# A two-layer graph kernel: plain stores in place of accumulating ones, the longest lists sorted in blocks, and the weights in a stream of their own

## The chip, the cores and the metric

The kernel runs on one core of a Trainium2 chip. The metric is the device time of one execution in microseconds (us); lower is better. A core has five engines with a queue each: TensorE (PE in the profile, with its weight loads as PEld), VectorE (DVE), ScalarE (ACT), GpSimd (POOL) and SyncE (SP). Plain transfers are issued here from SP, indirect ones (rows picked by a list of indices) from POOL.

## The reference

16 graphs of 1024 nodes with 64 channels. `adj` is a 1024 x 1024 matrix per graph with few entries; row and column i have weights that fall with i, so the first nodes have long neighbour lists.

```python
# layer 0
h = jnp.maximum(_layernorm(x, axis=-1), 0.0)
deg = jnp.clip(jnp.sum(A, axis=2, keepdims=True), 1.0, None)
x = x + jnp.matmul(A / deg, h)
# layer 1
h = jnp.maximum(_layernorm(x, axis=-1), 0.0)
adj_d = _dilate_adj(adj, mask)           # lists over 10 long lose two neighbours, both ways
vals = jnp.where(valid[..., None], h[:, None, :, :], big)
sv = jnp.sort(vals, axis=2)              # each channel sorted over a node's neighbours
# agg = 0.25 q(0.25) + 0.5 q(0.5) + 0.25 q(0.75), interpolated quantiles of sv
out = h + agg
y = relu(out @ W1 + b1) @ W2 + b2
x = x + y * mask
```

## The kernel before

The work has two parts. In the **layered part** each graph ("batch") is read once in eight row blocks `at` of 128 x 1024. ACT takes the sign of each block (`signs`), DVE finds neighbours with MAX8 (`listing`), PE transposes the block (`transposes`) and multiplies it with the normalised input (`products`). DVE then adds the input and leaves x after layer 0 in the tile `row`, at columns from `X1` on; `channels` normalises it into the first columns of `row`, stores the x part to `out` (16 stores of 256 KB) and the first 66 columns to a table `tab` in DRAM. `endings` sorts nodes by list length and scatters each row of `row`, without its x part (100 floats), to `srt`, by eight indirect DMAs per batch from POOL.

After every four batches, `group` reads the records of `srt`, cuts lists into classes by length (15, 10, 8, 7, 6, 5, 4, 3, 2, 1 neighbours at most) and makes a `Job` of each class, with T tiles of 128 nodes. After the last batch `long_lists` does the same for the four longest kinds (88, 31, 24 and 20 neighbours). This last stretch, with the last groups' jobs and the long lists, I call the **tail**.

A job goes like this. `run` issues on POOL one gather per list place and tile (`places<-tab,idx`, 128 rows of 66 floats; `lplaces` for long lists), and an SP load of the nodes' own rows (`S<-srt`). When all gathers are in, `sort` runs on DVE: it marks removed neighbours (`rem`, `gone`, `ok`), counts (`valid`), sets up the quantile weights (`q`, `u`), puts a huge value in the removed places, and runs a sorting network of MIN and MAX operations (`network` lists them, `spread` orders them); ACT finishes the weights (`wu`); DVE multiplies them in (`prod`). `layers` then sums the weighted places by PE transposes into `pt`, ACT copies to `ot`, PE multiplies with W1 (`ps_small`), ACT applies bias and ReLU (`hid`), PE multiplies with W2 and adds the bias `b2` by one more small matmul per tile, ACT multiplies by the mask into `y`, and POOL scatters `y` to `out`, one indirect DMA per tile that adds to what the plain stores left there. A chunk of `layers` holds up to four tiles; there are 128 tiles and 56 chunks in all. Between two scatters to the same tensor in a row a small memset (`turn`) is put on POOL.

Who comes next is set by a planner (`Plan`). Every piece of work is a generator ("stream") that yields the engine it needs next and the earliest time by the planner's own cost estimates; the planner always takes the stream that can begin first, with ranks for ties. What it yields is only a position: DVE and POOL execute exactly in the order in which the planner wrote their instructions, while the order on PE, ACT and SP is set by the compiling layer. `SLACK` (2) and `LOOSE` (7) are margins that the planner adds behind a result of another engine, as in the scatter of y:

```python
yield "POOL", lambda: at(y) + LOOSE
rows = out_rows[:min(self.g + 1, NG) * GB * N, :]
scatter(rows, y[:, t, :], self.nodes_i[:, t:t + 1], scatters, OP.add)
```

All recorded instructions have one line in the profile, L225, that of the recording helper; they are told apart by the names of their tiles.

Of the kernel before, what the change touches and what calls it, by code (L numbers as in the profile page):

```python
# [9 lines left out]
F32 = mybir.dt.float32  # L10
# [30 lines left out]
LSUB = 8  # L41
MOST = 8
# [106 lines left out]
def network(n, width):  # L149

    count = -(-3 * (n - 1) // 4) + 1
    live = set(range(count))
    layers = []
    for layer in reversed(SHORT.get(n) or batcher(n)):
        kept = [(i, j, i in live, j in live) for i, j in layer if i in live or j in live]
        live.update(x for pair in kept for x in pair[:2])
        layers.append(kept)  # L160
    goes = iter(GOES.get(n, ()))
    rules = iter(GOES_LONG.get(n, "").split())
    at = [2] + [0] * (n - 1)
    ops = []
    for layer in reversed(layers):
        kinds, after = {}, {}
        rule = dict(zip(sorted({(at[i], at[j]) for i, j, _, _ in layer}), next(rules, "")))
        for i, j, lo, hi in layer:
            ai, aj = at[i], at[j]
            other = (0 if ai == 1 else 1) + (0 if aj == 1 else 2)  # L170
            to = int(rule.get((ai, aj)) or next(goes, other))
            results = [(OP.min, i, to & 1)] * lo + [(OP.max, j, to >> 1)] * hi

            results.sort(key=lambda r: r[2] == at[r[1]])
            after.update({i: 0, j: 0})
            for turn, (op, x, copy) in enumerate(results):
                kinds.setdefault((turn, op == OP.max, ai, aj, j - i, copy), []).append(i)
                after[x] = copy
        for x, copy in after.items():
            at[x] = copy  # L180
        for (_, is_max, *kind), left in sorted(kinds.items()):
            cover = grids_of if rule else runs_of
            ops.extend((OP.max if is_max else OP.min, *kind, run) for run in cover(left))
    return spread(ops, width), count, at


def spread(ops, width):

    left, order = list(ops), []
    clock, ready = 0.0, {}  # L190
    while left:
        best, reads, writes = None, set(), set()
        for k, (op, ai, aj, dist, copy, run) in enumerate(left):
            run = numbers(run)
            near = {(ai, i) for i in run} | {(aj, i + dist) for i in run}
            out = {(copy, i + (dist if op == OP.max else 0)) for i in run}
            if not (near & writes or out & (reads | writes)):
                begin = max(clock, *(ready.get(key, 0.0) for key in near))
                if best is None or begin < best[0]:
                    best = begin, k, out  # L200
            reads |= near
            writes |= out
        begin, k, out = best
        clock = begin + 0.07 + len(numbers(left[k][5])) * width * 1.04e-3
        ready.update((key, clock + 0.15) for key in out)
        order.append(left.pop(k))
    return order
# [156 lines left out]
def list_path(ctx, tc, x, adj, nodemask, w1, b1, w2, b2, out, go):  # L364
# [12 lines left out]
    R0 = W  # L377
    X1 = RW = R0 + REC
# [64 lines left out]
    b2_sb = consts.tile([1, CO], F32, name="b2_sb")  # L443
    nc.sync.dma_start(b2_sb, b2.rearrange("(o c) -> o c", o=1))
# [110 lines left out]
    def beginnings(pool, now):  # L555

        for b, st in enumerate(batch):
            now[0] = b
            yield "DVE", lambda: max(known(st, "xt", "mrow"), room("h0", 3), room("row", 4))
            mrow_f = new(tiny, [NT, P], F32, "mrow_f", 2)  # L560
            nc.vector.tensor_copy(mrow_f, st["mrow"])

            h0 = new(pool, [P, NT, C + 1], F32, "h0", 3, users=2)
            nc.vector.memset(h0[:, :, C:], 1.0)
            row = st["row"] = new(pool, [P, NT, X1 + C], F32, "row", 4, users=1)
            nc.vector.memset(row[:, :, C:W], -1.0)
            yield from normed(h0[:, :, :C], st["xt"])
            st["h0"] = h0
            yield "PE", lambda: max(at(mrow_f), room("ps_small", 3))
            pm = new(ps_s, [P, HALF], F32, "ps_small", 3, users=1)  # L570
            nc.tensor.transpose(pm[:, :NT], mrow_f, ident[:NT, :NT])
            yield "ACT", lambda: at(pm)
            nc.scalar.copy(row[:, :, RW - 1], pm[:, :NT])
            nc.scalar.copy(row[:, :, RW - 2], row_f)
            free(pm)
# [79 lines left out]
    def products(pool, now):  # L655


        for b, st in enumerate(batch):
            now[0] = b
            for hf in range(2):  # L660
# [25 lines left out]
                x1 = st["row"][:, hf * BPH:(hf + 1) * BPH, X1:]  # L686
# [13 lines left out]
    def channels(pool, now):  # L700

        for b, st in enumerate(batch):
# [3 lines left out]
            yield from normed(row()[:, :, :C], row()[:, :, X1:])  # L706

            nc.sync.dma_start(out[b].rearrange("(t p) c -> p t c", p=P), row()[:, :, X1:])
# [5 lines left out]
    def endings(pool, now):  # L714

        first = lambda rank: rank - 3000
        for b, st in enumerate(batch):
# [55 lines left out]
            for t in range(NT):  # L773
                yield "POOL", lambda: max(at(to), at(row)) + LOOSE if "normed" in st else INF, first
                scatter(srt[g], row[:, t, :RW], to[:, t:t + 1], sorts[g])
# [10 lines left out]
    def scatter(dst, src, idx, others, op=OP.bypass):  # L786
        if plan.last is others:
# [3 lines left out]
            in_=src, in_offset=None, compute_op=op,  # L791
# [7 lines left out]
    class Job:  # L799
# [3 lines left out]
        def __init__(self, pool, n, T, keys, idx, node, mask, nodes_i, table, S, g, name="places",  # L803
                     bufs=4, rank=0):
            self.__dict__.update(locals())
            self.short = pool is gat

        def run(self):
# [10 lines left out]
            if short:  # L819
                mine = self.S  # L820
                self.S = new(pool, [P, T, W], F32, "S", 4, users=1)
                nc.sync.dma_start(self.S, mine)
            for t in range(T):
                for k in range(n - 1):
# [4 lines left out]
                    progress["ahead"] -= 1  # L829
            yield "DVE", lambda: max(  # L830
# [11 lines left out]

        def sort(self):
            n, T, pool, short, A, S = self.n, self.T, self.pool, self.short, self.A, self.S
            name = "" if short else "l"
            bufs = 2 if short else 1
            rem = new(pool, [P, n - 1, T, 2], F32, name + "rem2", bufs)
            nc.vector.tensor_tensor(
                rem, A[:, 1:, :, C:],
                self.node.unsqueeze(1).unsqueeze(3).to_broadcast([P, n - 1, T, 2]), OP.is_equal,  # L850
            )
            gone = new(pool, [P, n - 1, T], F32, name + "gone", bufs)
            nc.vector.tensor_tensor(gone, rem[:, :, :, 0], rem[:, :, :, 1], OP.max)
            ok = new(pool, [P, n - 1, T], F32, name + "ok", bufs)
            nc.vector.scalar_tensor_tensor(
                ok, self.keys.rearrange("p t k -> p k t"), 0.0, gone, op0=OP.is_gt,
                op1=OP.subtract,
            )
            valid = new(pool, [P, T], F32, name + "valid", bufs)
            nc.vector.tensor_reduce(valid, ok.rearrange("p k t -> p t k"), AX.X, OP.add)  # L860

            ops, count, copies = network(n, T * C)
            K = len(QUANTILES)
            q = new(pool, [P, K, T], F32, name + "q", bufs)
            nc.vector.tensor_tensor(
                q, taus.unsqueeze(2).to_broadcast([P, K, T]),
                valid.unsqueeze(1).to_broadcast([P, K, T]), OP.mult,
            )
            u = new(pool, [P, K, count, T], F32, name + "wu", 1)
            nc.vector.tensor_tensor(  # L870
                u, col_f[:, :count].unsqueeze(1).unsqueeze(3).to_broadcast([P, K, count, T]),
                q.unsqueeze(2).to_broadcast([P, K, count, T]), OP.subtract,
            )
            vals = A[:, 1:, :, :].rearrange("p k t w -> p (k t) w")[:, :, :C]
            nc.vector.scalar_tensor_tensor(
                vals,
                gone.rearrange("p k t -> p (k t)").unsqueeze(2).to_broadcast([P, (n - 1) * T, C]),
                HUGE, vals, op0=OP.mult, op1=OP.add,
            )
# [5 lines left out]
            yield "ACT", lambda: at(u) + SLACK  # L885
            nc.scalar.activation(u, u, AF.Abs)
            nc.scalar.activation(u, u, AF.Relu, bias=wt0, scale=-QUANTILES[0][1])
# [17 lines left out]
            begin = plan.clock["DVE"]  # L905
            for op, ai, aj, dist, copy, run in ops:
                each = numbers(run)
                near = [(ai, i) for i in each] + [(aj, i + dist) for i in each]
                soon = max(done.get(key, begin) for key in near)
# [15 lines left out]
            yield "DVE", lambda: at(u) + SLACK, self.later  # L925
# [38 lines left out]
        def layers(self, terms, sources):  # L964

            T, R = self.T, terms[0][0].shape[1]
            yield "PE", lambda: max(at(*sources) + LOOSE, room("y", 4), room("pt", 2))
            y = new(mlp, [P, T, CO], F32, "y", 4, users=1)
            for t0 in range(0, T, 4):
# [27 lines left out]
                pv = py[:, :len(ts) * CO].rearrange("p (t c) -> p t c", c=CO)  # L997
                for i, t in enumerate(ts):
                    nc.tensor.matmul(
                        pv[:, i, :], hid[:, i * P:(i + 1) * P], w2_sb, start=True, stop=False  # L1000
                    )
                    nc.tensor.matmul(pv[:, i, :], ones_f[:1, :], b2_sb, start=False, stop=True)
                yield "ACT", lambda: at(py) + SLACK
                for i, t in enumerate(ts):
                    nc.scalar.activation(
                        y[:, t, :], pv[:, i, :], AF.Copy, scale=self.mask[:, t:t + 1]
                    )
                free(py)
            for t in range(T):
                yield "POOL", lambda: at(y) + LOOSE  # L1010
                rows = out_rows[:min(self.g + 1, NG) * GB * N, :]
                scatter(rows, y[:, t, :], self.nodes_i[:, t:t + 1], scatters, OP.add)
# [3 lines left out]
    def group(g):  # L1016
# [107 lines left out]
        for i, ts in enumerate(classes):  # L1124
# [4 lines left out]
                nodes_i[:, sl], table, tiles[:, sl, :W], g,  # L1129
# [396 lines left out]
```

## Time and profile before

| | |
|---|---|
| median of 3 runs | 1586.0 us (1583.88 to 1586.02) |
| the profiled execution's own time | 1823.34 us |
| its span | 1821.4 us |
| granted TensorE clock in it | 0.653 |
| busy PE, DVE, ACT, POOL | 825.6, 1240.1, 609.3, 1050.8 us |
| indirect DMAs on POOL: gathers `places`, `lplaces` | 496 of 998 ns, 163 of 1049 ns |
| scatters to `srt`, to `out` | 128 of 1011 ns, 124 of 1678 ns and 4 of 1626 ns |
| last scatter to `srt` | begins at 988.4 us |

Groups of instructions in the profile read: line, engine, operation, output<-inputs, count, then busy us and mean ns of one, then the idle time of the engine just before them and what ended it. In the view of waits a line reads: who waited, for whom, us in total, times, longest. In the order of time: start, duration, engine, line, operation, and in brackets the idle time before it. The profiled execution takes longer than the timed runs; durations of single instructions are its own.

### The profile page before, as it was taken

The page shows a single profiled execution, that of the slowest core. Times are in us where ns is not written, and L with a number is a line of the kernel's source. Part 1 is how long each engine was busy: PE and PEld are TensorE (multiplying, and loading weights), DVE is VectorE, ACT ScalarE, POOL GpSimd, SP SyncE. Part 2 cuts the span into 40 slices and gives each one's busy share as a digit, 9 for nine tenths or more (in the row PEclk, how much of TensorE's full clock was granted, in tenths as well). Part 3 has the DMA queues.
Part 4 walks back from the last instruction along what each step waited for, and adds up shares of the span by engine and source line. Part 5 has one row for each costly group of instructions (what it writes and reads, how often), then busy time and mean ns, then how long its engine had stood idle before and what let it go on. Part 6 is the DMA issues. An engine that isn't in the chain of part 4 may idle for free. (4 is left out here: it accounts for less than half of the span.)

```text
span 1821.4 us, 15210 instructions
## 1 busy us (share of the span) xinstructions
PE 825.6 (45%) x3336; PEld 533.0 (29%) x3336; DVE 1240.1 (68%) x4046; ACT 609.3 (33%) x1874; POOL 1050.8 (58%) x1144
## 2 busy tenths in 40 slices
PE   5767822365686572563685000110031366253364
PEld 3333411233444341232354000100021245242343
DVE  7865858475788486678642889339497678896622
ACT  8877653245655464444442000000010111010011
POOL 0112263636467655555758766567656788575757
PEclk8978855675798675775885555555555567555656
DMA  5544741233444353353222211101111112111112
GB/s 170 163 133 122 199 125 31 48 101 81 121 134 112 58 134 91 90 138 73 56 48 49 43 43 34 23 17 22 28 24 28 18 26 20 23 30 23 24 18 17
DMA packets 147941, 124.89 MB, mean 69 GB/s; under 512 B 117715, under 2 KB 117843, under 8 KB 147843
## 3 DMA queue, kind: packets, MB, share of 16 engines
q1 hardware_dynamic: 102818, 86.58, 16.8%
q0 software_dynamic: 45024, 37.28, 12.2%
q14 instruction: 71, 0.57, 0.1%
q8 instruction: 28, 0.46, 0.1%
HBM read 104.51 MB, written 19.28 MB: 68 GB/s over the span
## 5 line engine op out<-in xcount | busy, mean ns | idle before, releaser
L225 POOL DMA_INDIRECT places<-tab,idx x496 | 495.0, 998 | 165.1 <-issue 140.2
L225 PE MATMUL pt<-ident,prod 128*128 128x128 f32 (+1 forms) x736 | 161.8, 384 | 569.4 <-DVE prod L225 294.5
L225 POOL DMA_INDIRECT out_dram<-y,nodes_i x124 | 208.0, 1678 | 186.8 <-ACT y L225 127.4
L225 PEld LDWEIGHTS pt<-ident,prod 128*128 128x128 f32 (+1 forms) x736 | 134.2, 267 | 605.3 <-issue 389.7
L225 POOL DMA_INDIRECT srt<-row,to x128 | 129.4, 1011 | 259.0 <-ACT row L225 223.5
L225 PE MATMUL pt<-ident,at 128*128 128x128 f32 x1024 | 190.0, 334 | 179.6 <-ACT att L225 72.1
L225 PE MATMUL ps_small<-att,h 128*65 128x512 f32 x512 | 259.0, 652 | 17.7 <-ACT h L225 10.3
L225 PEld LDWEIGHTS pt<-ident,at 128*128 128x128 f32 x1024 | 143.5, 171 | 236.5 <-ACT att L225 97.7
L225 POOL DMA_INDIRECT lplaces<-tab,lidx x163 | 171.0, 1049 | 49.7 <-issue 49.1
L225 ACT COPY att<-pt 128x512 f32<-128x512 f32 x256 | 142.9, 583 | 155.7 <-remote 84.2
L225 DVE MAX8 rec<-sg 128x8 f16<-128x256 f16 x512 | 180.1, 414 | 9.5 <-remote 5.2
L225 ACT ACTIVATE wu<-wu 128x39 f32<-128x39 f32 (+9 forms) x40 | 9.4, 234 | 431.7 <-DVE wu L225 168.8
L225 ACT ACTIVATE sg<-at 128x1024 f16<-128x1024 f32 x128 | 134.9, 1055 | 31.7 <-DMA at<-in_adj_dram 15.3
L225 DVE TENSOR_TENSOR sg<-sg,keyed 128x1024 f16<-128x1024 f16 x128 | 87.4, 683 | 65.5 <-issue 33.4
L225 PEld LDWEIGHTS ps_small<-att,h 128*65 128x65 f32 x512 | 75.4, 153 | 149.4 <-issue 126.5
L225 ACT COPY ot<-pt 128x128 f32<-128x128 f32 (+3 forms) x56 | 22.4, 400 | 246.7 <-remote 128.2
L225 PE MATMUL ps_small<-ot,w_sb 128*128 128x128 f32 (+3 forms) x112 | 55.9, 593 | 104.7 <-ACT ot L225 72.6
L225 PE MATMUL ps_small<-w_sb,hid 128*128 128x64 f32 x256 | 72.5, 376 | 52.6 <-ACT hid L225 25.1
L225 DVE TENSOR_TENSOR other<-places,other 128x64 f32<-128x64 f32 (+6 forms) x204 | 69.5, 341 | 35.6 <-remote 16.3
L225 PEld LDWEIGHTS ps_small<-w_sb,hid 128*128 128x128 f32 x256 | 53.6, 258 | 80.5 <-ACT hid L225 40.3
L225 DVE TENSOR_TENSOR rem<-places,recs 128x30 f32<-128x30 f32 (+9 forms) x40 | 7.3, 182 | 101.7 <-DMA places<-tab,idx 90.0
L225 POOL MEMSET turn<- 128x1 f32 x204 | 76.2, 373 | 0.1
(206 smaller groups left out, 1712.2 us busy)
## 6 DMA issues: line engine op xcount, KB each, us to landing
at<-in_adj_dram SPq DMA_DIRECT2D x128, 512.0 KB
places<-tab,idx POOLq DMA_INDIRECT x496
tab<-row SPq DMA_DIRECT2D x16, 264.0 KB
xt<-in_x_dram SPq DMA_DIRECT2D x16, 256.0 KB
out_dram<-row SPq DMA_DIRECT2D x16, 256.0 KB
lplaces<-tab,lidx POOLq DMA_INDIRECT x163
recs<-srt SPq DMA_DIRECT2D x4, 544.0 KB
srt<-row,to POOLq DMA_INDIRECT x128
```

Source lines behind the costliest of these rows:

```text
L225: ins = getattr(self._engine, op)(*args, **kwargs)
```

## The change

- The tile `row` and the sorted table `srt` now carry x after layer 0 as well (164 floats a row, was 100). The plain stores of `row` to `out` are gone.
- `layers` fetches x of its nodes: short jobs by an SP load from `srt` into the tile `y` (40 loads in all), long lists from their `S` tile. `y` has five buffers (was four).
- The last step moves from ACT to DVE: y = PSUM x mask + x in one operation per tile, and the scatter to `out` is a plain one. The bias `b2` comes by one matmul per chunk, of up to 256 columns, ahead of the W2 matmuls (one of 64 columns per tile behind each before).
- Lists of more than `BLOCK` (32) places, that is the longest kind, start their sort as a stream of its own, in blocks of 32 places: each block is prepared when its gathers are in (`prepared`), and network operations that stay in one block are kept apart.
- The two ACT operations for the weights become a stream of their own (`weigh`); the network no longer follows them in the planner's order.

The core of the diff:

```diff
-def network(n, width):
+def network(n, width, block=None):
...
+        apart = block and all(i // block == j // block for i, j, _, _ in layer)
...
+                kind = i // block if apart else 0, turn, op == OP.max, ai, aj, j - i, copy
+                kinds.setdefault(kind, []).append(i)
...
+    ready = {(0, i): 1.3 * block * (i // block + 1) for i in range(n)} if block else {}
+    return spread(ops, width, ready), count, at
...
-    R0 = W
-    X1 = RW = R0 + REC
+    X1 = W
+    R0 = X1 + C
+    RW = R0 + REC
...
-            nc.sync.dma_start(out[b].rearrange("(t p) c -> p t c", p=P), row()[:, :, X1:])
...
-                scatter(srt[g], row[:, t, :RW], to[:, t:t + 1], sorts[g])
+                scatter(srt[g], row[:, t, :], to[:, t:t + 1], sorts[g])
...
-                self.S = new(pool, [P, T, W], F32, "S", 4, users=1)
-                nc.sync.dma_start(self.S, mine)
+                self.S = new(pool, [P, T, C], F32, "S", 4, users=1)
+                nc.sync.dma_start(self.S, mine[:, :, :C])
+                self.residual = mine[:, :, X1:R0]
+            self.blocks = [(1, n)] if n <= BLOCK else [
+                (max(k, 1), min(k + BLOCK, n)) for k in range(0, n, BLOCK)
+            ]
+            self.fetched = [INF] * len(self.blocks)
+            if len(self.blocks) > 1:
+                plan.add(self.sort(), 100 * NG)
...
+        def weigh(self, u):
+
+            yield "ACT", lambda: at(u) + SLACK
+            nc.scalar.activation(u, u, AF.Abs)
+            nc.scalar.activation(u, u, AF.Relu, bias=wt0, scale=-QUANTILES[0][1])
+            self.weighed = at(u)
...
+            def prepared(c):
+
+                if c:
+                    yield "DVE", lambda: fetched[c] + SLACK, self.later
...
+                    plan.add(self.weigh(u), -1000)
...
+                while len(begins) <= max(of(i) for _, i in near):
+                    yield from prepared(len(begins))
...
-            yield "DVE", lambda: at(u) + SLACK, self.later
+            yield "DVE", lambda: self.weighed + SLACK, self.later
...
+            y = new(mlp, [P, T, CO], F32, "y", 5, users=1)
+            x1 = y
+            if self.short:
+                nc.sync.dma_start(x1, self.residual)
+            else:
+                x1 = self.S[:, :, X1:R0]
...
+                nc.tensor.matmul(
+                    py[:, :len(ts) * CO], ones_f[:1, :], b2_sb[:, :len(ts) * CO],
+                    start=True, stop=False,
+                )
                 for i, t in enumerate(ts):
                     nc.tensor.matmul(
-                        pv[:, i, :], hid[:, i * P:(i + 1) * P], w2_sb, start=True, stop=False
+                        pv[:, i, :], hid[:, i * P:(i + 1) * P], w2_sb, start=False,
+                        stop=(i == len(ts) - 1),
                     )
-                    nc.tensor.matmul(pv[:, i, :], ones_f[:1, :], b2_sb, start=False, stop=True)
-                yield "ACT", lambda: at(py) + SLACK
+                yield "DVE", lambda: at(py) + LOOSE
                 for i, t in enumerate(ts):
-                    nc.scalar.activation(
-                        y[:, t, :], pv[:, i, :], AF.Copy, scale=self.mask[:, t:t + 1]
+                    nc.vector.scalar_tensor_tensor(
+                        y[:, t, :], pv[:, i, :], self.mask[:, t:t + 1], x1[:, t, :],
+                        op0=OP.mult, op1=OP.add,
                     )
...
-                rows = out_rows[:min(self.g + 1, NG) * GB * N, :]
-                scatter(rows, y[:, t, :], self.nodes_i[:, t:t + 1], scatters, OP.add)
+                scatter(out_rows, y[:, t, :], self.nodes_i[:, t:t + 1], scatters)
```

## The prediction

> **What bounds the kernel now.** I read the page's slices and costliest groups first, then the busy time of the two parts of the run, then POOL's and VectorE's (DVE's) waits in the second part, then the order of time around one wait.
>
> The slices and three groups:
>
> ```profile
> DVE  7865858475788486678642889339497678896622
> ACT  8877653245655464444442000000010111010011
> POOL 0112263636467655555758766567656788575757
> ...
> L225 POOL DMA_INDIRECT places<-tab,idx x496 | 495.0, 998 | 165.1 <-issue 140.2
> ...
> L225 POOL DMA_INDIRECT out_dram<-y,nodes_i x124 | 208.0, 1678 | 186.8 <-ACT y L225 127.4
> ...
> L225 POOL DMA_INDIRECT srt<-row,to x128 | 129.4, 1011 | 259.0 <-ACT row L225 223.5
> ```
>
> No engine is full for the whole run. From slice 22 on ScalarE (ACT) is nearly empty, the adjacency is done, and POOL and DVE share what is left. Busy time of the two parts:
>
> ```profile
> 0.00:990.00 990.00, 590.65 (x2345) 348.17 (x2346) 674.76 (x2252) 545.58 (x1670) 488.47 (x600) 0.73 0.40 104
> 990.00:1822.00 832.00, 234.97 (x993) 184.81 (x991) 565.32 (x1794) 63.71 (x204) 562.36 (x545) 0.56 0.17 26
> ```
>
> (Columns: length; busy of PE, weight loads, DVE, ACT, POOL; clock, DMA share, GB/s.) In the 832 us after 990, the tail, POOL and DVE are busy 562 and 565 us. POOL's waits there:
>
> ```profile
> POOL out_dram L225 <- ACT y L225: 77.2, 10, 14.0
> POOL places L225 <- issue: 67.1, 220, 0.3
> POOL lplaces L225 <- issue: 49.1, 161, 0.3
> POOL out_dram L225 <- ACT prod L225: 21.1, 2, 10.6
> ```
>
> The "issue" gaps are 0.30 us between gathers: they belong to the gather, whose start-to-start step is 1.25 us. Real waits are 77.2 + 21.1 + 4.4 (a third line) = 103 us for y, and some 25 us for other things. So in the tail POOL works or waits for y. DVE's longest waits there are for gathers: 80.3 us for `places` and 26.9 us for the 88 gathers of the longest list. They are two halves of one loop: gather, sort, layers, scatter.
>
> The step of a scatter to `out`, at the very end, and of one to `srt`:
>
> ```profile
> 1808.60 1.57 POOL L225 DMA_INDIRECT out_dram<-y,nodes_i  x1 [0.19 <-issue]
> 1809.57 0.71 POOL L225 MEMSET turn<- 128x1 f32 x1
> 1810.47 1.57 POOL L225 DMA_INDIRECT out_dram<-y,nodes_i  x1 [0.19 <-issue]
> ```
> ```profile
> 412.56 0.97 POOL L225 DMA_INDIRECT srt<-row,to  x1 [0.19 <-ACT row L225]
> 413.53 0.12 POOL L225 MEMSET turn<- 128x1 f32 x1
> 413.84 0.97 POOL L225 DMA_INDIRECT srt<-row,to  x1 [0.19 <-issue]
> ```
>
> 1.87 us against 1.28 us: an accumulating scatter costs POOL 0.6 us more than a plain one. And one wait for y:
>
> ```profile
> 1721.04 0.50 ACT L225 COPY prod<-S 128x384 f32<-128x384 f32 x1
> 1742.50 0.26 ACT L225 ACTIVATE wu<-wu 128x72 f32<-128x72 f32 x1 [20.95 <-DVE wu L225]
> 1742.79 0.35 ACT L225 ACTIVATE wu<-wu,wt 128x72 f32<-128x72 f32 x1
> 1747.38 0.58 ACT L225 COPY ot<-pt 128x512 f32<-128x512 f32 x1 [4.23 <-remote]
> ```
>
> PE had finished that `pt` at 1734.9, but in ACT's queue the weights of the next job stood ahead of the `ot` copy, and those waited for the next job's gathers; POOL then waited 12.0 us for y, until 1756.5.
>
> **What the Trainium skill says.** "DMA: Bandwidth & Descriptors", section "SWDGE vs HWDGE vs iDMA": descriptors of DMAs issued from GpSimd are computed by software on its cores, and accumulating during a DMA exists on that path only. The trace agrees as far as it goes: each indirect DMA holds POOL about 1 us, the accumulating kind 1.6. "Perfetto Trace Analysis", section "GPSIMD Engine Instruction": take such instructions by start-to-start spacing, not by reported duration. The trace agrees: the 1.57 us of a scatter overlaps the memset after it, so I use steps. "Perfetto Trace Analysis", section "Optimizing Scalar/DVE Operations": access costs DVE about 60 ns in SBUF and 125 ns in PSUM. The nearest rows hardly show it: 128x64 operations with `other` in PSUM take 228 ns, with `lplaces` in SBUF 225 ns.
>
> **The change part by part**, against the profiled execution's own 1823.3 us (span 1821.4). The median of the runs, 1586.0, is 0.870 of that; I let savings shrink alike.
>
> 1. *Plain scatters.* Built order: 82 of the 128 scatters now lie after the last `srt` scatter (77 before), with 399 gathers (406 before). Tail, POOL: (77 x 1.88 + 406 x 1.25) - (82 x 1.28 + 399 x 1.25) = 652 - 604 = 48 us less. I take 0.85 of it, **-41**, since part would otherwise lie under DVE's sorting; ends -25 and -48. The other 46 scatters save 0.6 x 46 = 28 us in a part where POOL idles 223.5 us for `row`, so they are counted in item 6.
>
> 2. *Waits for y.* In the built order after, ACT's queue in the tail has `ot` and `hid` of a job ahead of the next job's weights, so waits like that at 1756 go. The 72 bias matmuls that are left out (128 to 56, in two passes each, 0.62 us the pair at the tail's clock) shorten the layers of a four-tile chunk by about 1.4 us: three pairs out, the one left four times wider. Late next is the layers' own chain, some 14 us for four tiles (at 1727: transposes 7.5, copy 0.6, first matmul 2.1, activation 0.7, second matmuls 2.5). I take a third of 103 us, **-35**; ends 0 and -80.
>
> 3. *The longest list in blocks.* Its first 31 places can be sorted while the other 57 are fetched. The most it can give is DVE's 26.9 us; but DVE has other work in line, and in that stretch POOL itself stood 10.6 and 12.9 us for y. **-10**; ends 0 and -27. The weights' own stream changes only where `wu` stands on ACT: counted in 2.
>
> 4. *Added DVE work.* 128 last steps from PSUM at 0.14 (step of independent 128x64 operations) to 0.23 us: 18 to 29 us. Each of the two further blocks adds three small operations of 0.25 us and splits the large one; 20 more network operations and 5 memsets at 0.07 us fixed cost: some 4 us. Two thirds fall in the tail; half of all is taken as covered by waits for gathers, **+12**; ends +4 and +33.
>
> 5. *New waits on DVE.* 56 chunks end in an operation that waits for PE, and everything behind it on DVE waits too. In the built tail y of a job mostly stands right after its `prod`, ahead of the next job's first operation: 14 to 20 us of standing, where DVE now stands for gathers (13.7, 25.0, 9.7 us at the end). One place has no such cover: eleven y operations (three chunks) stand just ahead of `rev`, the start of the long lists, after which DVE is 88% busy; there DVE already waited 10.9 us, and 20 would be some 10 more. **+20** in all; ends 0 and +150.
>
> 6. *The layered part.* Sixteen 256 KB stores of `row` go; 40 loads of y and 3 of the bias come on SP, 27 issues more at about 0.4 us. In the built order y loads stand between adjacency loads, and each waits for a y buffer (five now); a late scatter would hold the adjacency behind it. `srt` rows grow from 400 to 656 bytes, S loads lose 8 bytes in 264; DMA is 40% busy there. The 128 operations of 0.31 us leave ACT, 55% busy there: hidden. POOL's 63.6 us of waits ahead of scatters there (50.2 for y, 13.4 for `row`) and item 1's 28 us are mostly cover for something else: **-10**; ends -40 and +30.
>
> Sum: -41 - 35 - 10 + 12 + 20 - 10 = **-64**, so 1759; times 0.870: **1530 us**.
>
> **The rivals.**
> *DVE's new waits decide (slower).* In the layered part PE has transposes to do, and from DVE's `prod` to y it took 13 us (T=2, at 407), 26 (T=1, at 419), 30 (T=4, at 466) and 72 (T=6, at 563). If DVE stands there, listing and the next batches' `srt` scatters are late. Without item 5 the sum is -84; spread over 56 waits that is gone at 1.5 us uncovered each. At 3 us each (+168) the run is at 1907, or 1659. For it: DVE's order is fixed and 68% full there. Against it: y is put many instructions after its `prod` in that part.
> *The loop closes (much faster).* If the waits go on both sides, the tail falls towards its floors: POOL 604 + 36 for the other DMAs and slow gathers = 640; DVE 565 + 20, plus 74 us of small gaps (832 - 565 - 193 of waits in the list), 659. With 690 it is 142 shorter; with 20 from the layered part 1661, or 1445. Against it: two engines at 93% each hardly ever meet without waits.
> *Plain scatters cost the same.* If the 1.88 us come from writing to `out` and not from accumulating, item 1 falls away: 1800, or 1566. Against it: `srt` is also a scatter to DRAM.
>
> **How the numbers follow.** Chances: forecast 0.48 (own range 1480 to 1570), loop closes 0.20, scatters as dear 0.11 (of which 0.05 within the bound), DVE's waits 0.21. So faster by over 0.2% 0.74, within 0.2% 0.05, slower 0.21. 0.2% is 3.2 us, about what a measurement of this kernel can tell from no change. The range takes half of each outer case: **1450 to 1615**.
>
> **What would show it.** Right: the scatter to `out` steps 1.28 us; POOL's waits ahead of it in the tail are under 70 us, and now for DVE; DVE's wait for the longest list is gone; the last `srt` scatter stays near 989 us. Wrong: y on DVE with waits on PE of over 100 us in all; the part up to the last `srt` scatter longer than before; SP standing on y; or a scatter that still steps 1.9 us.

## The result, and the profile after

The change makes the kernel **slower by 2.4%**: 1622.9 us (median of 4 runs) against 1585.3 us, ratio 1.0236 (95% interval 1.022 to 1.0253). The prediction was 1530 us, faster.

One thing is needed to understand the numbers below: in each set of runs taken together the kernel before takes either about 1585 us or about 1829 us, so every ratio is taken to the kernel before as it ran beside, and I speak of "the 1585 group" and "the 1829 group". The groups go with the chip: wherever the record names it, the first ran on one chip (number 9) and the second on two others (4 and 15). The profiled execution before has the time of the second group, the timed runs before and everything shown of after that of the first. So the kernel before was profiled again (experiment `again`, span 1588.8 us), and after is compared with that.

The page of after: the slices, and the groups of scatters and of the new last step.

```profile
DVE  6767899999997999987478999999889988432221
ACT  7889886465676454565300000000001100000000
POOL 0222247666677775778766577777687776443543
...
L230 POOL DMA_INDIRECT srt<-row,to x128 | 129.7, 1013 | 183.3 <-ACT row L230 158.9
L230 POOL DMA_INDIRECT out_dram<-y,nodes_i x124 | 125.8, 1015 | 154.0 <-DVE y L230 108.7
...
L230 DVE SCALAR_TENSOR_TENSOR y<-ps_small,recs,y 128x64 f32<-128x64 f32 x124 | 28.0, 276 | 91.1 <-PE ps_small L230 90.8
```

DVE is on the whole fuller than in the page of before up to slice 34, and then both engines empty out: in the last six slices, 243 us, DVE has digits of 4 down to 1 and POOL of 5 to 3. The busy time of the two parts, split at the last scatter to `srt`, of after and then of the kernel before in its second profile (length; busy of PE, weight loads, DVE, ACT, POOL; clock, DMA share, GB/s):

```profile
0.00:810.00 810.00, 540.50 (x2308) 303.91 (x2308) 683.69 (x2314) 531.52 (x1619) 467.28 (x595) 0.81 0.47 130
810.00:1622.10 812.10, 187.99 (x884) 148.10 (x884) 585.43 (x1893) 44.95 (x127) 515.78 (x549) 0.56 0.14 30
```
```profile
0.00:831.00 831.00, 567.10 (x2380) 334.91 (x2380) 672.64 (x2252) 547.15 (x1681) 493.42 (x599) 0.80 0.48 124
831.00:1588.80 757.80, 221.79 (x956) 175.75 (x956) 564.61 (x1794) 60.48 (x193) 565.77 (x545) 0.56 0.20 29
```

The layered part got 21 us shorter. The whole loss is in the tail: 54 us longer, although POOL has 50 us less to do there. What POOL and DVE wait for in after's tail (who, for whom, us in total, times, longest):

```profile
POOL out_dram L230 <- DVE y L230: 108.7, 12, 22.7
...
POOL out_dram L230 <- DVE rem L230: 11.2, 2, 7.7
```
```profile
DVE rem L230 <- DMA places<-tab,idx: 88.8, 5, 24.0
DVE y L230 <- PE ps_small L230: 80.9, 12, 15.6
...
DVE lrem L230 <- DMA lplaces<-tab,lidx: 3.5, 1, 3.5
```

POOL's saved work has turned into waits for y: 120 us, against 28.6 us in the kernel before (20.1 + 8.5, below). The order of time shows them. One job near the end of after, first DVE, then POOL (start, duration; idle before it in brackets):

```profile
1524.38 0.20 DVE L230 TENSOR_TENSOR rem<-places,recs 128x36 f32<-128x36 f32 x1 [23.96 <-DMA places<-tab,idx]
...
1533.79 0.55 DVE L230 TENSOR_TENSOR prod<-other,w 128x384 f32<-128x384 f32 x1
1549.96 0.86 DVE L230 SCALAR_TENSOR_TENSOR y<-ps_small,recs,y 128x64 f32<-128x64 f32 x4 [15.62 <-PE ps_small L230]
...
1569.87 0.18 DVE L230 TENSOR_TENSOR rem<-places,recs 128x24 f32<-128x24 f32 x1 [16.70 <-DMA places<-tab,idx]
```
```profile
1526.51 1.31 POOL L230 DMA_INDIRECT places<-tab,idx  x1 [0.30 <-issue]
1550.53 0.99 POOL L230 DMA_INDIRECT out_dram<-y,nodes_i  x1 [22.71 <-DVE y L230]
1551.82 0.98 POOL L230 DMA_INDIRECT out_dram<-y,nodes_i  x1 [0.18 <-issue]
...
1558.16 0.98 POOL L230 DMA_INDIRECT places<-tab,idx  x1 [0.31 <-issue]
```

Nothing overlaps: DVE waits 24 us for the gathers, sorts for 10 us, waits 15.6 us for the layers; POOL has issued only four gathers of the next job, the last at 1526.51, when it comes to the scatters of this one, and waits 22.7 us for y with the next job's other gathers behind them. Then DVE waits for those. The scatters themselves step 1.29 us, as predicted.

### The profile page after: what moved, and what is told of

It reads as the page before. It is cut to its first block, busy times and chain, and to the rows that moved or that the text cites. A ratio compares the mean times of both kernels' runs of the same rounds, so it can differ in the third digit from the quotient of the medians.

```text
span 1622.1 us, 14952 instructions
## 1 busy us (share of the span) xinstructions
PE 728.5 (45%) x3192; PEld 452.0 (28%) x3192; DVE 1269.1 (78%) x4207; ACT 576.5 (36%) x1746; POOL 983.1 (61%) x1144
## 3 DMA queue, kind: packets, MB, share of 16 engines
q1 hardware_dynamic: 102696, 86.46, 19.1%
## 5 line engine op out<-in xcount | busy, mean ns | idle before, releaser
L230 POOL DMA_INDIRECT places<-tab,idx x496 | 508.3, 1025 | 156.0 <-issue 145.4
L230 PE MATMUL pt<-ident,prod 128*128 128x128 f32 (+1 forms) x736 | 152.8, 369 | 640.9 <-DVE prod L230 591.7
L230 PEld LDWEIGHTS pt<-ident,prod 128*128 128x128 f32 (+1 forms) x736 | 125.9, 253 | 671.1 <-DVE prod L230 409.3
L230 POOL DMA_INDIRECT out_dram<-y,nodes_i x124 | 125.8, 1015 | 154.0 <-DVE y L230 108.7
L230 PE MATMUL pt<-ident,at 128*128 128x128 f32 x1024 | 165.6, 306 | 75.0 <-ACT att L230 61.0
L230 PEld LDWEIGHTS pt<-ident,at 128*128 128x128 f32 x1024 | 126.8, 155 | 120.7 <-ACT att L230 85.1
L230 ACT COPY att<-pt 128x512 f32<-128x512 f32 x256 | 141.1, 582 | 19.1 <-PE pt L230 18.0
L230 DVE SCALAR_TENSOR_TENSOR y<-ps_small,recs,y 128x64 f32<-128x64 f32 x124 | 28.0, 276 | 91.1 <-PE ps_small L230 90.8
L230 DVE TENSOR_TENSOR places<-places,other 128x64 f32<-128x64 f32 (+2 forms) x208 | 62.5, 309 | 4.9
L230 DVE TENSOR_TENSOR long_other<-lplaces 128x512 f32<-128x512 f32 (+6 forms) x130 | 65.6, 537 | 0.5
L230 DVE TENSOR_TENSOR lplaces<-long_other 128x512 f32<-128x512 f32 (+6 forms) x116 | 61.7, 566 | 0.1
```

Source lines behind the costliest of these rows:

```text
L230: ins = getattr(self._engine, op)(*args, **kwargs)
```

## The experiments

Theory A: the cause is the **order**. `prepared` sets the planner's own time (`plan.own`) without looking when the fetches arrive, and `note` leaves the readiness of inputs out whenever `own` is set:

```python
if self.own is not None:
    self.clock[engine] = max(self.clock[engine], self.own)
...
    *(self.ready.get(v.tensor.name, 0.0) for v in rest if self.own is None),
```

So the planner lets a job be sorted before its gathers are in. For the job above it reckons the sort from 1392 us and the last gather until 1442 us (its own reckoning while the kernel is built, no measured times). Everything behind the sort is then planned too early, y seems ready by the time the gathers end, and the scatters are written ahead of the next job's gathers. The old preparation was noted in the ordinary way. Theory B: the cause is DVE's **waits for y**, the rival of the prediction.

**`again`**: the kernel before, unchanged.

> The kernel before, unchanged, profiled and timed once more. The prediction worked on one profiled execution of 1823.3 us and shrank every saving by 0.870 to the median of 1586. If that execution was an ordinary one with its times stretched, this one again has a span near 1820, with DVE about 68% busy and the same waits. If it was an odd one, with stalls that the timed runs don't have, this span is near 1584, DVE about 78% busy, and the waits that items 2, 3 and 6 were sized on (103 us of POOL for y, 26.9 us of DVE for the longest list, 223.5 us of POOL for `row`) are other numbers.

1585.3 us, span 1588.8 us: the first profile was not an ordinary one. In the tail POOL waits for y, and DVE for gathers, like this:

```profile
POOL out_dram L225 <- ACT y L225: 20.1, 9, 7.7
...
POOL out_dram L225 <- ACT prod L225: 8.5, 1, 8.5
```
```profile
DVE rem L225 <- DMA places<-tab,idx: 64.0, 9, 20.7
DVE lrem L225 <- DMA lplaces<-tab,lidx: 38.6, 2, 36.2
```

28.6 us for y instead of the 103 us that item 2 was sized on; 38.6 us for long lists' gathers instead of 26.9.

**`plan_clock`**: one line of the changed kernel.

```diff
-                plan.own = plan.clock["DVE"] + 0.1
+                plan.own = max(plan.clock["DVE"], fetched[c]) + 0.1
```

> The changed kernel with one line of its planner altered: a job's preparation is planned to begin no earlier than its fetches arrive (it is a number for the planning alone; every instruction is the same, only their order on DVE and POOL differs). Theory A, the order: in the built order of the changed kernel only 4, 4, 4 and 0 gathers of later jobs stand between the last gather of each of the four last jobs and its scatters, where the kernel before has 22, 17, 5 and 0, so gathers, sorting, layers and scatters run one after the other; with the line it is 14, 17, 5 and 0. POOL's five waits of 19.2, 22.1, 22.7, 12.5 and 14.3 us for y at the end (91 us) should halve, and the time fall by 40 to 80 us, to 1540 to 1580. Theory B, DVE's new waits: y on DVE waits for PE wherever it is put; the 90.8 us of those waits stay within 20 and the time stays within 10 us of 1623.

1562.5 us, 0.985 of before (0.9815 to 0.9885): 60 us faster than after, with the same work. It is faster than both kernels, 1.5% faster than before. Its tail in waits, POOL then DVE:

```profile
POOL out_dram L230 <- DVE y L230: 39.6, 11, 11.8
```
```profile
DVE y L230 <- PE ps_small L230: 80.0, 16, 11.5
DVE rem L230 <- DMA places<-tab,idx: 25.9, 3, 11.4
```

DVE's waits for y are the same 80 us as in after's tail; the waits that went are POOL's for y and DVE's for gathers. That is theory A; B is out as the cause of the loss. The line moves instructions on DVE and on POOL, and their shares in the gain are not told apart. The end itself, the last five jobs, in after and then in `plan_clock` (columns as above):

```profile
1410.00:1613.00 203.00, 59.02 (x220) 42.54 (x220) 49.35 (x131) 13.69 (x32) 86.03 (x106) 0.55 0.08 16
```
```profile
1430.00:1559.00 129.00, 53.56 (x222) 38.49 (x221) 49.06 (x131) 13.59 (x32) 84.83 (x107) 0.61 0.14 28
```

49 us of DVE and some 85 us of POOL in both, done in 129 us instead of 203. That is 74 us. The spans differ by 62.5, so some 12 net are lost earlier in the run: the layered part of `plan_clock` is 26 us longer (last `srt` scatter at 834.9 against 808.9 us).

**`before_clock`**: the early clock in the kernel before.

```diff
             rem = new(pool, [P, n - 1, T, 2], F32, name + "rem2", bufs)
+            plan.own = plan.clock["DVE"] + 0.1
...
+            plan.own += 0.3
...
+            plan.own = None
```

> The kernel before, with the early planning clock of the changed kernel's preparation put in (planned times only; the same instructions in another order). Theory A: 1586 plus 30 to 90 us, with the scatters of the last jobs ahead of the next job's gathers and POOL's waits for y at the end longer by as much. Theory B: the order matters only through y on DVE, which this kernel does not have: within 10 us of 1586.

1703.0 us, 1.0732 of before (1.0695 to 1.0768): 117 us slower, more than A expected and far from B. This kernel has no y on DVE, so the order alone does it. POOL's waits for y in its tail, 28.6 us in `again`:

```profile
POOL out_dram L225 <- ACT y L225: 114.1, 9, 24.0
```

The layered part is longer too (last `srt` scatter at 884.9 against 829.9 us), by about half of the loss: the early clock misplaces jobs everywhere, not only at the end.

**`stores_alone`**: `plan_clock` with the longest list sorted whole, without blocks, and with the weights inline, that is in the sort's own stream.

```diff
-BLOCK = 32
+BLOCK = 128
...
-                    plan.add(self.weigh(u), -1000)
...
+                if c == len(blocks) - 1:
+                    yield from self.weigh(u)
```

> Plain stores with the last step on DVE alone: lists sorted whole, the weights in the sort's own stream as before, and the planned clock waiting for the fetches. Theory A: items 1 and 2 hold without the early clock, 20 to 60 us faster than before, 1525 to 1565; the scatter to `out` steps 1.28 us. Theory B: DVE's new waits for PE take the gain back, 1580 to 1640, with over 80 us of DVE's waits for y.

1560.0 us, 0.9839 (0.9803 to 0.9876). The gain is as large as with all three parts of the change: blocks and the weights' stream add nothing that shows in the 1585 group.

**`accumulate`, `last_step_act`, `no_blocks`, `weights_inline`**, first run in the 1829 group, and the first three again beside `plan_clock_2` in the 1585 group. Their edits to `plan_clock`, in that order (`no_blocks` and `weights_inline` are the two halves of `stores_alone`; `accumulate` leaves out the plain stores of x, and `last_step_act` the addition of x):

```diff
-    def scatter(dst, src, idx, others):
+    def scatter(dst, src, idx, others, op=OP.bypass):
...
-                scatter(out_rows, y[:, t, :], self.nodes_i[:, t:t + 1], scatters)
+                scatter(out_rows, y[:, t, :], self.nodes_i[:, t:t + 1], scatters, OP.add)
```
```diff
-                yield "DVE", lambda: at(py) + LOOSE
+                yield "ACT", lambda: at(py) + SLACK
...
-                    nc.vector.scalar_tensor_tensor(
-                        y[:, t, :], pv[:, i, :], self.mask[:, t:t + 1], x1[:, t, :],
-                        op0=OP.mult, op1=OP.add,
+                    nc.scalar.activation(
+                        y[:, t, :], pv[:, i, :], AF.Copy, scale=self.mask[:, t:t + 1]
```

> The version with the mended planning clock, its scatters to `out` made accumulating again (so `out` is y added to what was there): the same instructions in the same order on every engine, so the run prices item 1 alone. The step of a scatter should go from 1.28 back to 1.87 us, POOL's busy time up by about 128 x 0.6 = 77 us. Item 1 as predicted: 41 us slower than the version without, 1604. Rival: POOL is not what the tail waits for once y is on DVE (DVE is 81% busy): under 15 us slower. Other rival: POOL is the bound everywhere: 77 us slower.

> The version with the mended planning clock, its last step back on ScalarE (y = the PSUM value times the mask; the addition of the old row is left out), all else kept: it prices items 4 and 5. DVE loses 124 + 4 operations (28 us) and 83 us of waits for PE. If those waits decide: 40 us faster, near 1520. If they lie beside waits for gathers and for y: within 12 us of 1562, with DVE's waits for gathers longer by most of the 83 us.

> The version with the mended planning clock with the longest list sorted whole (BLOCK = 128). Item 3: 10 us slower than 1562, with one wait of DVE of some 27 to 40 us for the longest list's gathers (36.2 us in the second profile of the kernel before). Rival: the wait is only exchanged for others, within 6 us.

> The version with the mended planning clock, the weights' two ScalarE operations back in the sort's own stream. The prediction counted nothing for them alone: within 6 us of 1562. Rival: they hold the `ot` copies on ScalarE's queue again, 15 us or more slower, with POOL's waits for y over 60 us.

Measured in the 1829 group, against the kernel before there: 0.9918 (0.9886 to 0.995), 1.0044 (1.0014 to 1.0074), 1.0073 (1.0039 to 1.0107) and 1.0199 (1.0163 to 1.0236). The expected times were for the other group, and `plan_clock` was missing beside them, so by themselves these ratios decide nothing.

> The version with the mended planning clock again, as the reference for the next three, which ran first where the kernel before took 1829 us: 0.985 of the kernel before if the ratio of the first run holds where this one runs, whatever the absolute time.

> The accumulating scatters (`out` is y added to what was there) in the same order of instructions, now beside the version without. Item 1: 41 us slower than that version (2.6%). Rival, DVE the bound: under 15 us (1%). Rival, POOL the bound everywhere: 77 us (4.9%).

> The last step on ScalarE without the addition of the old row, now beside the version with it on DVE. Items 4 and 5 as predicted (12 + 20): 32 us faster, 2%. Rival: the waits and the added work on DVE lie beside other waits: within 12 us (0.8%). Where the kernel before took 1829 us this version was not faster (1842), which speaks for the rival.

> The longest list sorted whole, now beside the version in parts. Item 3: 10 us slower (0.6%). Rival: within 6 us; where the kernel before took 1829 us it was 0.7% slower than that kernel, so over 1% slower than the version in parts is possible too, if parts free DVE for the short lists.

| 1585 group, run together | us | of before (interval) |
|---|---|---|
| `plan_clock_2` | 1566.1 | 0.9878 (0.9857 to 0.99) |
| `accumulate_2` | 1599.2 | 1.0086 (1.0061 to 1.011) |
| `last_step_act_2` | 1559.8 | 0.9855 (0.9829 to 0.9881) |
| `no_blocks_2` | 1568.8 | 0.9912 (0.9886 to 0.9937) |

(The ratios compare runs taken side by side, and are not always exactly the quotients of the medians.) The accumulating scatters cost **33 us** in one and the same order of instructions. The last scatters of `accumulate_2`, then of `plan_clock_2`:

```profile
1586.74 1.57 POOL L230 DMA_INDIRECT out_dram<-y,nodes_i  x1 [0.20 <-issue]
1587.72 0.70 POOL L230 MEMSET turn<- 128x1 f32 x1
1588.61 1.57 POOL L230 DMA_INDIRECT out_dram<-y,nodes_i  x1 [0.19 <-issue]
```
```profile
1553.32 0.95 POOL L230 DMA_INDIRECT out_dram<-y,nodes_i  x1 [0.19 <-issue]
1554.27 0.12 POOL L230 MEMSET turn<- 128x1 f32 x1
1554.58 0.96 POOL L230 DMA_INDIRECT out_dram<-y,nodes_i  x1 [0.19 <-issue]
```

1.87 against 1.26 us a step. POOL's busy time differs by 81 us, so four tenths of it reach the end; 21 us only take the place of POOL's waits for y in the tail (45.7 us in `plan_clock_2`, 24.7 in `accumulate_2`). Of the 35 us between the two spans, 16 have come by the last `srt` scatter (852.8 against 836.8 us), and only 19 are added in the tail.

The last step on DVE costs **6 us** by the medians (0.4%; the intervals overlap). Without it DVE's waits for y are gone, and what DVE then waits for in the tail is this, against 25.9 us in `plan_clock_2`:

```profile
DVE rem L230 <- DMA places<-tab,idx: 80.0, 8, 27.5
```

54 of the 83 us of waits that y had there come back as waits for gathers. Blocks are worth 2.7 us, with overlapping intervals: nothing that I can call shown. `stores_alone` and `no_blocks_2`, which ran at different times, differ by the weights alone: with the weights inline 0.9839 (0.9803 to 0.9876), with their own stream 0.9912 (0.9886 to 0.9937). With the longest list sorted whole, inline is not slower in this group.

**`plan_clock_3`, `weights_inline_3`, `weights_inline_2`, `before_bias`, `dve_margin`, `pool_margin`**, all in the 1829 group. `before_bias` is the kernel before with the merged bias matmuls of the diff; the two margins are these lines of `plan_clock`, each alone:

```diff
-                yield "DVE", lambda: at(py) + LOOSE
+                yield "DVE", lambda: at(py) + 2 * LOOSE
...
-                yield "POOL", lambda: at(y) + LOOSE
+                yield "POOL", lambda: at(y) + 2 * LOOSE
```

> The kernel before with the bias matmuls merged to one in each chunk (128 to 56) and nothing else. Item 2's part of it: about 1.4 us off the layers of each four-tile chunk, where POOL's waits for y in the tail are 28.6 us in the second profile of the kernel before: at most 15 us faster. Rival: PE's time lies off the path, within 5 us of 1585.

> The version with the mended planning clock with the weights in the sort's own stream, where the kernel before takes about 1585 us if it runs on such a chip again: within 6 us of 1565 by the prediction (nothing counted for it alone); rival: 15 us or more slower, as 1868 against 1829 for the kernel before in its first run would suggest (2.0% over that kernel).

> The version with the mended planning clock with y on DVE planned 14 instead of 7 us after its matmuls (planned times only). If DVE's 83 to 86 us of waits for y decide anything, most of them go and the time falls by 15 us or more; if they lie beside waits for gathers, within 6 us of 1565.

> The same with the scatters to `out` planned 14 instead of 7 us after y (planned times only), y on DVE as it was. POOL's waits for y (52 and 57 us in two profiles) should fall under 30 us. If POOL's order decides, 10 to 25 us faster, near 1545; if DVE does, within 6 us of 1565.

> The version with the mended planning clock. Where the kernel before takes about 1585 us: 0.985 to 0.988 of it again. Where it takes about 1829 us, PE stands still for some 350 us in all, waiting for nothing that the trace shows, and a wait for y on DVE then holds DVE too: theory, no gain left, 1.00 to 1.02 of the kernel before; rival, the gain of 20 us stays, 0.985 to 0.99.

> The same with the weights in the sort's own stream. Where the kernel before takes about 1585 us: within 6 us of the version above by the prediction; rival, 15 us or more slower. Where it takes about 1829 us it ran at 1.020 and 1.021 of it, and should again.

| 1829 group | us | of before (interval) |
|---|---|---|
| `before_bias` | 1822.9 | 0.9928 (0.9895 to 0.9962) |
| `dve_margin` | 1843.0 | 1.0065 (1.0038 to 1.0092) |
| `pool_margin` | 1895.0 | 1.0340 (1.0277 to 1.0404) |
| `weights_inline_2` | 1870.8 | 1.0211 (1.0163 to 1.0259) |
| `plan_clock_3` | 1825.2 | 1.0008 (0.9975 to 1.0041) |
| `weights_inline_3` | 1874.6 | 1.0246 (1.0176 to 1.0316) |

There the gain of the mended clock over before is gone, and the accumulating version (0.9918, not run beside it, and on another chip of the group) is not slower than the plain one (1.0008). What differs from the 1585 group is seen first on PE. Its waits in `plan_clock_3`, and POOL's for y:

```profile
PE pt L230 <- issue: 104.7, 32, 15.7
PE ps_small L230 <- issue: 62.1, 14, 14.7
```
```profile
POOL out_dram L230 <- DVE y L230: 191.8, 25, 25.8
```

PE stands still 46 times, 167 us in all, for nothing that the trace shows; the profiles of the 1585 group have no such line among PE's waits. Releasers are missing from the records of the 1829 group (12,804 semaphore updates in `plan_clock_3`, 24,670 in `plan_clock_2`), so a part of these may be waits for something. The longest of `accumulate` ends like this:

```profile
660.41 0.59 ACT L230 COPY att<-pt 128x512 f32<-128x512 f32 x1 [21.52 <-remote]
661.05 1.12 PE L230 MATMUL pt<-ident,at 128*128 128x128 f32 x4 [24.71 <-issue]
```

PE runs nothing from 636.3 to 661.05 us, where the same matmuls stand 2.6 us apart in `accumulate_2`. It is not PE alone: ACT runs nothing for 21.5 us, SP issues nothing from 633.1 to 660.40, and DVE takes 19.1 us (641.29 to 660.41) for the operations that take it 6.0 us in `accumulate_2` (553.59 to 559.57). Only POOL keeps its step (1.25 us from gather to gather). (The 350 us in my expectation were too much: one wait of 157.6 us in the first profile of before is its long wait for `prod`, 155.6 us in the second.) A stop delays a y and POOL waits longer for it, so POOL's own speed should count for less there; that is argued, not shown. The merged bias gives 0.7% of the kernel before (0.4% to 1.1%), within the expected 15 us, though that was expected of the 1585 group. The wider margins are no gain: `pool_margin` is some 3% slower than `plan_clock_3`, `dve_margin` 0.6% with intervals that just overlap; they ran only there and not beside it, so for the 1585 group it stays open. Putting the weights inline costs 2.7% over `plan_clock_3` (1874.6 / 1825.2), but the order on DVE and POOL moves with it, so this is not the price of the two ScalarE operations alone; with blocks there is no run of it in the 1585 group.

## Why the prediction was wrong

The failed step is in **item 5**, an overlap that was not there. It said that in the tail "y of a job mostly stands right after its `prod`" and costed this as "14 to 20 us of standing, where DVE now stands for gathers". In after DVE stands for both, near the end 15.6 us for y and then 16.7 us for the next job's gathers, because those wait behind the scatters of that same y. So POOL's waits for y, which item 2 let fall by a third, rose from 28.6 to 120 us, and the order that does this, put at nothing, costs 60 us (after against `plan_clock`). The place was seen, its meaning was not. I looked at what the wait covers on DVE, and counted in the built order how many scatters lie in the tail, but not how many gathers of the next job stand between a job's last gather and its scatters. There are 4, 4, 4 and 0 for the last four jobs, against 22, 17, 5 and 0 before and 14, 17, 5 and 0 in `plan_clock`. The Trainium skill has the rule behind this in "PSUM — Partial Sum Buffer", section "Engine vs sequencer instructions": ScalarE's, VectorE's and GpSimd's queues are strict FIFO. The trace agrees: the scatter at 1550.53 keeps the gather at 1558.16 behind it for 22.7 us while POOL has nothing else to do. The cause, the lines with `plan.own`, was there in the changed kernel to be read; I read the order that it produced and not the reckoning that produced it.

Item by item, us in the 1585 group (predicted savings there times 0.870, as the prediction had it):

| item | predicted | measured |
|---|---|---|
| 1 plain scatters | -36, in the tail | -33 in all, a little over half of it in the tail (`accumulate_2`) |
| 3 longest list in blocks | -9 | -3 (`no_blocks_2`), not separable from nothing |
| 4 + 5 last step on DVE, its waits | +28 | +6 (`last_step_act_2`) |
| 2 + 6 waits of POOL for y, layered part | -39 | +12, what is left over of the -17.6 of `plan_clock_2` |
| the early planning clock | not there | +60 (after against `plan_clock`) |

(The two sets of runs put the version with the mended clock at -24 and at -18 us; with the first, -24 + 60 = 36 of after's 38.)

- **Item 1** was right in mechanism: the step went from 1.87 us to between 1.26 and 1.29. Its size agrees by luck. It took 0.85 of the tail's saving and counted the rest under item 6, as mostly cover; between `accumulate_2` and `plan_clock_2` POOL saves 47 us in the tail and 34 before it, and 19 and 16 of these reach the end.
- **Item 2** was mis-sized at its source: a third of 103 us, from a profile of the 1829 group. The second profile has 28.6 us, so 35 was not to be had. That the weights on ACT hold up y is not borne out in the 1585 group: inline, they cost nothing in `stores_alone`. What the merged bias gives there wasn't measured.
- **Item 3**: the wait did go (3.5 us in after, 38.6 before), and DVE's other waits took its place.
- **Items 4 and 5**: DVE has 32 us more to do (1269.1 against 1237.3), near the upper end of the 22 to 33 that the step's terms add up to; added work and new waits lie beside waits for gathers more than I allowed.
- **Item 6**: SP does stand on y, 177.5 us in 33 waits for scatters to land (123.5 us of it before 810 us), as it could have; the last `srt` scatter came 21 us earlier all the same. Between the kernels of one group that scatter lies anywhere from 803.1 (`stores_alone`) to 884.9 us (`before_clock`), so the order of the plan moves this part more than any cost in the item. The +12 is not traced to a cause.
- **The factor 0.870** was the wrong use of a good observation. A profile 237 us above the timed runs isn't the same run stretched: the work is nearly the same (DVE busy 1240.1 and 1237.3 us, PE 825.6 and 788.9) and most of the difference is stops. These two lines of the first profile's waits of PE said so, and I passed over them:

```profile
PE pt L225 <- issue: 285.6, 32, 157.6
...
PE ps_small L225 <- issue: 64.9, 23, 8.3
```

The slower rival had the right sign by another mechanism: DVE's waits for y, its cause, are 80 us with the loss and without it. Of the signs named ahead, "POOL's waits ahead of it in the tail are under 70 us" was the one that told: 120 us, and under 50 with the mended line.

## What to carry to other kernels

Where a planner writes the order, a change to what it is told about time is a change to the kernel: compare its clock for each moved step with what the step waits for, and count what stands between a producer and its consumer in each strict queue, not only how many instructions there are. A wait on one engine that "lies beside another wait" was harmless here only where the next piece of work was already under way on the other engines. And if the profiled time is far above the timed runs, first find which waits make the difference, and size no item on those.

## What was not expected of the hardware

Wherever the chip is on record, the same kernel took 1585 us on one and 1829 on two others, with nearly the same busy times. In the stop at 661 us of `accumulate` PE, ACT and SP stand for over 20 us and DVE runs at a third of its pace, while POOL goes on; the trace names no reason, and what stops them isn't settled. The ranking of kernels is not the same in both groups: plain scatters are worth 2.1% in one, and in the other, by runs that were not side by side, nothing.
